# Layer 3's input halves stored by quarter as [w, sample], and the result read back with a step

## The chip, the cores and the metric

The kernel runs on one core of one Trainium2 chip. A core has five engines with a queue each: PE (TensorE, matrix products into PSUM), DVE (VectorE), ACT (ScalarE), POOL (GpSimd[...]) and SP (SyncE, which here only starts DMA transfers). The metric is the device time of one execution in microseconds. Before the change the median of three runs is 3868.43 us (3868.01 to 3870.23).

## What is computed

The input x has 8192 samples of 8 channels by 16 rows by 16 columns, in f32. Four layers run one after the other; each normalises its input by groups of two channels (`_gn`), applies an operator, and adds the result to its input:

```
x = x + L0(_gn(x))    # a tensor-train operator on [8, 16, 16], plus bias
x = x + L1(_gn(x))    # 3x3 convolution, batch norm over all samples, relu
x = x + L2(_gn(x))    # 3x3 convolution on values rounded to int8 steps, one scale for the whole tensor
x = x + L3(_gn(x))    # 3x3 convolution with binarized weights, edge padding
```

The change touches layer 3 alone:

```
w = binarize(weight)                  # sign(weight) * mean(|weight|) of its output channel
xp = pad(x, 1 on each side, mode='edge')
out = conv(xp, w) + bias
```

"Edge" padding means that the column left of column 0 repeats column 0, and the column right of column 15 repeats column 15.

## The kernel before

**Layout.** A tile holds 128 samples. Its 128 partitions are the pairs (channel, row), 8 x 16, and its 2048 words per partition are [sample b, column w], with w innermost. So there are 64 tiles. A convolution over channels and rows is a product with a 128x128 banded matrix, and its three column offsets are three products that add up in one PSUM bank. A bank holds 512 f32 words per partition, which is a quarter of a tile: 32 samples by 16 columns (`NQ = 4`, `QS = 32`, `BANK = 512`).

**Stages.** Four passes go over all tiles: layer 0 with the convolution of layer 1 (to about 2650 us), the batch norm and the statistics of layer 2 (to about 3090 us), and then layer 2's convolution together with layer 3 (from about 3095 us to the end). The change lies in the last pass. All engine instructions go through helper `InOrder`, which keeps them in the order in which the program text issues them, so each engine is a strict list; the profile shows the helper's line, L43, for all of them, and rows are told apart by the names of their tiles.

**The last pass, one turn of its loop** (lines 969 to 989; names of tiles in brackets as the profile shows them). Each turn works on several tiles at different depth:

- PE: six products of layer 2 for the first half of a tile [pq], products that spread small statistics over all partitions [ps_a, ps_r, ps_o], six more for the second half [pq], sixteen that sum x and x squared [s], then 24 of layer 3 [pf]: twelve for the first half of the tile and twelve for the second. The twelve are two quarters, times two operands, times three column offsets.
- DVE: small statistics [diag_d, rows_d, mr, diag_e, rows_e], `finish` of the second half of layer 3 [reads pf], layer 2's addition [reads pq], `scale2` [v], the reduction of s and small steps [s_d, mv], `scale3` [t, which lives in the buffers sq and xh], `finish` of the first half of the next tile [reads pf].
- ACT: x squared [sq], the offset [c], layer 2's second half [bs<-pq], `edges3` [lo<-lo], `round2` [q<-v], `high3` [hi<-xh, hi<-sq], its edges [hi<-hi], `bias2` [bias].
- POOL: the second half of layer 2 added to x [<-bs], a power of four words [mv<-mv,mhalf], `low3` [lo<-sq,hi and lo<-xh,hi], and the offset added to x [<-c].

**How layer 3 feeds PE.** The scaled input t is split in two operands for PE: `high3` rounds t to the type fp32r [hi], and `low3` stores what is left, t - hi [lo]. Each has 18 columns per sample, [128 samples, 18], so that columns 0 and 17 can hold the repeated edges, which `edges` fills with 2 x 128 words. `layer3` then reads, for column offset n, 32 runs of 16 words that lie 18 words apart (`tv[:, :, n:n + W]`), and `finish` adds the PSUM result, times `scale3`, to x with one DVE instruction of 1024 words per half. The PSUM tiles [pc] of layers 2 and 3 come from one pool with two buffers, in turn: pq of the first half, pq of the second half, pf of the first half, pf of the second half. A product into a buffer waits until the engine that reads it, DVE or ACT, has read what it held. hi, lo and t have two buffers each; sq holds one square at a time.

Of the kernel before, what the change touches and what calls it, by code (L numbers as in the profile page):

```python
# [8 lines left out]
F32 = mybir.dt.float32  # L9
F32R = mybir.dt.float32r  # L10
# [3 lines left out]
ALU = mybir.AluOpType  # L14
# [4 lines left out]
P = 128  # L19
C, H, W = 8, 16, 16  # L20
# [4 lines left out]
NQ = 4  # L25
QS = P // NQ
BANK = QS * W
# [26 lines left out]
def tile_net(ctx: ExitStack, tc: tile.TileContext, xb, xt_in, pack0, pack1, pack2, out):  # L54
# [3 lines left out]
    pe, dve, act, pool = (InOrder(tc, e) for e in (nc.tensor, nc.vector, nc.scalar, nc.gpsimd))  # L58
# [74 lines left out]
    L = {}  # L133
# [129 lines left out]
    def samples(t):  # L263
        return t.rearrange("p (b w) -> p b w", w=W)

    def over_w(stat, a, b):

        return stat[:, a:b].unsqueeze(2).to_broadcast([P, b - a, W])
# [25 lines left out]
    with first as s:  # L294
        small = s.enter_context(tc.tile_pool(name="small1", bufs=3))
        wk = s.enter_context(tc.tile_pool(name="wk", bufs=2))
# [4 lines left out]
        T = [dict() for _ in range(NT)]  # L301
# [263 lines left out]
        for n in range(NT * NQ):  # L565
            t, q = divmod(n, NQ)
# [58 lines left out]
        t = NT - 1  # L625
# [83 lines left out]
    with tc.tile_pool(name="p2", bufs=2) as p2, tc.tile_pool(name="ps2", bufs=2, space=PSUM) as ps2:  # L709
        T = T2  # L710
# [115 lines left out]
    with ExitStack() as s:  # L826
        wk = s.enter_context(tc.tile_pool(name="wk3", bufs=2))
# [5 lines left out]
        T = [dict() for _ in range(NT)]  # L833
# [17 lines left out]
        def halves(t):  # L851
            return t.rearrange("p (h n) -> p h n", h=2)
# [70 lines left out]
            T[i]["t"] = t  # L923


        def edges(t):
            act.copy(t[:, :, 0:W + 2:W + 1], t[:, :, 1:W + 1:W - 1])

        def high3(i):
            T[i]["hi"] = hi = wk.tile([P, P, W + 2], F32R, name=f"hi_{i}", tag="hi")  # L930
            act.copy(hi[:, :, 1:W + 1], samples(T[i]["t"]))
            edges(hi)

        def low3(i):
            hi = T[i]["hi"]
            T[i]["lo"] = lo = wk.tile([P, P, W + 2], F32R, name=f"lo_{i}", tag="lo")
            pool.tensor_tensor(lo[:, :, 1:W + 1], samples(T[i].pop("t")), hi[:, :, 1:W + 1].bitcast(F32), ALU.subtract)
            x = samples(T[i]["x"])
            pool.tensor_tensor(x, x, over_w(T[i].pop("c"), 0, P), ALU.add)

        def edges3(i):
            edges(T[i]["lo"])

        def layer3(i, h):
            pc = ps_c.tile([P, 2, BANK], F32, name=f"pf_{i}_{h}", tag="pc")
            for m, t in enumerate(("hi", "lo")):
                for k in range(2):
                    q = 2 * h + k
                    tv = T[i][t][:, q * QS:(q + 1) * QS]
                    for n in range(3):  # L950
                        pe.matmul(samples(pc[:, k]), L["sign3"][:, n], tv[:, :, n:n + W],
                                  start=(m == n == 0), stop=(m == 1 and n == 2))
            T[i]["pf", h] = pc

        def finish(i, h):
            x = halves(T[i]["x"])[:, h]
            pc = T[i].pop(("pf", h)).rearrange("p k n -> p (k n)")
            dve.scalar_tensor_tensor(x, pc, L["scale3"], x, ALU.mult, ALU.add)
            if h == 1:
                nc.sync.dma_start(out[order[i]], T[i]["x"])  # L960
                T[i].clear()
# [7 lines left out]
        for i in range(-FIRST, NT + 4):  # L969
            at(i + AHEAD, lambda j: j >= AHEAD and load3(j))  # L970
            at(i + FIRST, rows2)
            at(i - 1, rows3)
            at(i - 3, finish, 1)
            at(i, square3)
            at(i + 1, layer2, 0)
            spread(i + FIRST, i - 1)
            at(i - 1, offset3)
            at(i + 1, layer2, 1)
            at(i + FIRST, scale2)
            at(i, stats3)  # L980
            at(i - 1, scale3)
            at(i - 2, edges3)
            at(i + 2, round2)
            at(i - 1, high3)
            at(i + 2, bias2)
            at(i - 1, low3)
            at(i - 2, layer3, 0)
            at(i - 2, finish, 0)
            at(i - 2, layer3, 1)
# [69 lines left out]
```

## Time and profile before

| what | value |
|---|---|
| median of three runs | 3868.43 us |
| span of the profiled execution | 3866.3 us |
| PE, DVE, ACT, POOL busy over the span | 3616.3, 3408.0, 2510.8, 3044.2 us |
| steady part of the last pass | 3123 to 3838 us, 715 us |
| PE, DVE, ACT, POOL busy in it | 710.89, 657.07, 554.13, 695.93 us |
| granted TensorE clock in it | 1.00 |
| share of the DMA engines' time in it | 0.43 |
| one turn of the loop (one tile) | 11.55 us (layer 3's products start at 3399.89, 3411.44, 3422.99 us) |

How to read it: matrix products are pipelined, so the time that the profile gives to one (433 ns) is not its share of PE's time; the distance from one start to the next is. A column "idle before" gives how long an engine stood still ahead of a group of instructions and whose end it waited for. A loop in which each engine has a fixed list settles to the length of its slowest cycle of waits, and that cycle may run through several engines.

### The profile page before, as it was taken

The page shows a single profiled execution, that of the slowest core. Times are in us where ns is not written, and L with a number is a line of the kernel's source. Part 1 is how long each engine was busy: PE and PEld are TensorE (multiplying, and loading weights), DVE is VectorE, ACT ScalarE, POOL GpSimd, SP SyncE. Part 2 cuts the span into 40 slices and gives each one's busy share as a digit, 9 for nine tenths or more (in the row PEclk, how much of TensorE's full clock was granted, in tenths as well). Part 3 has the DMA queues.
Part 4 walks back from the last instruction along what each step waited for, and adds up shares of the span by engine and source line. Part 5 has one row for each costly group of instructions (what it writes and reads, how often), then busy time and mean ns, then how long its engine had stood idle before and what let it go on. Part 6 is the DMA issues. An engine that isn't in the chain of part 4 may idle for free.

```text
span 3866.3 us, 52820 instructions
## 1 busy us (share of the span) xinstructions
PE 3616.3 (94%) x16326; PEld 2131.0 (55%) x16326; DVE 3408.0 (88%) x6316; ACT 2510.8 (65%) x2672; POOL 3044.2 (79%) x3101
## 2 busy tenths in 40 slices
PE   7899999999999999999999999996665589999998
PEld 4566666666666666666666666662211145555555
DVE  6988888888888888888888888877998889999997
ACT  4566666666666666666666666665665477777775
POOL 4687777777777777777777777766887679999998
PEclk8999999999999999999999999998776699999999
DMA  5678788787887878878788787757999624444432
GB/s 206 208 249 269 254 264 269 250 268 254 264 270 250 269 253 263 269 252 265 255 263 269 254 265 255 257 185 283 425 424 425 280 90 183 185 183 183 180 153 98
DMA packets 210665, 960.93 MB, mean 249 GB/s; under 512 B 44880, under 2 KB 45136, under 8 KB 109776
## 3 DMA queue, kind: packets, MB, share of 16 engines
q1 hardware_dynamic: 173664, 692.22, 48.3%
q0 software_dynamic: 36288, 264.26, 22.9%
q8 instruction: 131, 2.15, 0.2%
q14 instruction: 150, 1.23, 0.1%
q10 hardware_dynamic: 432, 1.08, 0.1%
HBM read 578.84 MB, written 378.54 MB: 248 GB/s over the span
## 4 chain that ended last, share of the span: by engine, by line
PE 84%; DVE 7%; DMA 4%; issue 2%; POOL 1%; ACT 1%; POOLq 0%; DVEq 0%; SPq 0%; ACTq 0%
PE po L43 44%; PE pu L43 12%; PE pf L43 10%; PE pm L43 6%; PE pq L43 4%; PE s L43 3%; PE pc L43 3%; DVE top L43 3%; DMA yk<-y_d 1%; DVE ys L43 1%; DMA x_d<-xs 1%; DMA x_d<-xk 1%; DMA xk<-x_d 1%; DMA xs<-x_d 1%; DMA u<-x_d 1%
## 5 line engine op out<-in xcount | busy, mean ns | idle before, releaser
L43 PE MATMUL po<-u,core 128*128 128x512 f32 (+1 forms) x4112 | 1847.0, 592 | 1.9 <-DVE xs L43 1.9
L43 ACT COPY u<-pu 128x2048 f32<-128x2048 f32 x512 | 955.4, 1866 | 534.1 <-PE pu L43 534.0
L43 PEld LDWEIGHTS po<-u,core 128*128 128x128 f32 x4112 | 745.7, 190 | 740.4 <-issue 737.3
L43 PE MATMUL pu<-core2r,xl 128*128 128x256 f32 x4032 | 680.1, 311 | 11.3 <-DMA xl<-limb_d 11.3
L43 PEld LDWEIGHTS pu<-core2r,xl 128*128 128x128 f32 x4032 | 529.2, 189 | 134.1 <-issue 133.8
L43 POOL TENSOR_TENSOR bs<-bs,xh 128x512 fp32r<-128x512 f32 (+1 forms) x253 | 324.6, 1283 | 206.0 <-ACT xh L43 206.0
L43 POOL TENSOR_TENSOR v<-e 128x128 f32<-128x128 f32 x750 | 397.4, 541 | 0.0
L43 DVE TENSOR_TENSOR xs<-po,xs 128x512 f32<-128x512 f32 x256 | 177.0, 691 | 236.6 <-PE po L43 236.6
L43 ACT ACTIVATE m<-pm,b 128x128 f32<-128x128 f32 x250 | 91.7, 367 | 405.4 <-PE pm L43 405.4
L43 PEld LDWEIGHTS pm<-v,fast 128*128 128x128 f32 x2000 | 263.4, 192 | 129.9 <-issue 112.1
L43 POOL TENSOR_TENSOR e<-x1n,x 128x512 f32<-128x512 f32 x250 | 305.9, 1224 | 23.4 <-ACT x L43 16.1
L43 DVE TENSOR_TENSOR bs<-bs,stat 128x1024 f32<-128x1024 f32 x252 | 290.8, 1216 | 2.1
L43 POOL TENSOR_TENSOR xs<-xs,w 128x2048 f32<-128x2048 f32 x64 | 291.5, 4555 | 0.0
L43 PE MATMUL pm<-v,fast 128*128 128x128 f32 x2000 | 264.9, 276 | 9.6 <-DVE ends L43 9.6
L43 ACT ACTIVATE x<-x1n 128x512 f32<-128x512 f32 x500 | 246.9, 544 | 2.1 <-DVE x1n L43 2.1
L43 POOL TENSOR_TENSOR mv<-mv,mhalf 128x4 f32<-128x4 f32 x127 | 130.8, 1030 | 146.4 <-DVE mv L43 146.4
L43 PE MATMUL pf<-hi,sign 128*128 128x512 f32 x768 | 226.8, 433 | 0.0
L43 PE MATMUL pf<-lo,sign 128*128 128x512 f32 x768 | 219.5, 423 | 3.3 <-ACT lo L43 3.3
L43 POOL DMA_DIRECT2D xl<-limb_d x252 | 149.7, 594 | 87.5 <-ACT x L43 47.8
L43 POOL TENSOR_TENSOR v<-r 128x128 f32<-128x128 f32 x500 | 215.6, 447 | 0.0
L43 POOL TENSOR_TENSOR mvb<-mvb,mhalf 128x4 f32<-128x4 f32 x64 | 66.3, 1035 | 179.4 <-DVE mvb L43 174.6
L43 ACT ACTIVATE sq<-xs 128x2048 f32<-128x2048 f32 (+1 forms) x107 | 199.3, 1862 | 4.6 <-POOL xs L43 4.6
(289 smaller groups left out, 7180.4 us busy)
## 6 DMA issues: line engine op xcount, KB each, us to landing
xl<-limb_d POOLq DMA_DIRECT2D x252, 1024.0 KB, 7.4
x_d<-xs SPq DMA_DIRECT2D x76, 1024.0 KB, 8.4
bs<-in_xb SPq DMA_DIRECT2D x64, 1024.0 KB, 5.7
xs<-in_xt SPq DMA_DIRECT2D x64, 1024.0 KB, 7.6
limb_d<-xh SPq DMA_DIRECT2D x1008, 64.0 KB, 4.3
limb_d<-bs SPq DMA_DIRECT2D x1008, 64.0 KB, 5.1
y_d<-ys SPq DMA_DIRECT2D x60, 1024.0 KB, 8.0
u<-x_d SPq DMA_DIRECT2D x36, 1024.0 KB, 6.1
```

The source lines that it names most:

```text
L43: return self.tc.keep_in_program_order(op(*args, **kwargs))
```

## The change

The operands hi and lo are stored by quarter as [18 columns, 32 samples] in place of [128 samples, 18 columns]. A column offset n is then a shift by 32 n words, so that each product reads one run of 512 words. To get there, `high3` and `low3` read t with a step of 16 words (samples innermost) and write runs. The products' columns come out in the order [w, b], so `finish` reads PSUM with a step of 32 words to bring them back to [b, w]; it does so with one instruction per quarter, where it had one per half. The edges become runs of 32 words.

```diff
         def high3(i):
-            T[i]["hi"] = hi = wk.tile([P, P, W + 2], F32R, name=f"hi_{i}", tag="hi")
-            act.copy(hi[:, :, 1:W + 1], samples(T[i]["t"]))
+            T[i]["hi"] = hi = wk.tile([P, NQ, W + 2, QS], F32R, name=f"hi_{i}", tag="hi")
+            act.copy(hi[:, :, 1:W + 1], by_w(T[i]["t"]))
             edges(hi)
...
+        def by_w(t):
+            return t.rearrange("p (q b w) -> p q w b", q=NQ, w=W)
...
-            T[i]["lo"] = lo = wk.tile([P, P, W + 2], F32R, name=f"lo_{i}", tag="lo")
-            pool.tensor_tensor(lo[:, :, 1:W + 1], samples(T[i].pop("t")), hi[:, :, 1:W + 1].bitcast(F32), ALU.subtract)
+            T[i]["lo"] = lo = wk.tile([P, NQ, W + 2, QS], F32R, name=f"lo_{i}", tag="lo")
+            pool.tensor_tensor(lo[:, :, 1:W + 1], by_w(T[i].pop("t")), hi[:, :, 1:W + 1].bitcast(F32), ALU.subtract)
...
-                    tv = T[i][t][:, q * QS:(q + 1) * QS]
                     for n in range(3):
-                        pe.matmul(samples(pc[:, k]), L["sign3"][:, n], tv[:, :, n:n + W],
+                        tv = T[i][t][:, q, n:n + W].rearrange("p w b -> p (w b)")
+                        pe.matmul(pc[:, k], L["sign3"][:, n], tv,
                                   start=(m == n == 0), stop=(m == 1 and n == 2))
...
-            pc = T[i].pop(("pf", h)).rearrange("p k n -> p (k n)")
-            dve.scalar_tensor_tensor(x, pc, L["scale3"], x, ALU.mult, ALU.add)
+            pc = T[i].pop(("pf", h)).rearrange("p k (w b) -> p k b w", w=W)
+            for k in range(2):
+                v = samples(x[:, k * BANK:(k + 1) * BANK])
+                dve.scalar_tensor_tensor(v, pc[:, k], L["scale3"], v, ALU.mult, ALU.add)
```

## The prediction

> **What bounds the kernel now.** I read the stretches first, since only the last pass changes, then the chain of waits inside it, the rows by shape and last the waits. In a steady stretch of 100 us (columns: length, then busy time of PE, weight loads, DVE, ACT and POOL, clock, DMA share, GB/s):
>
> ```profile
> 3400.00:3500.00 100.00, 100.00 (x496) 59.28 (x497) 93.28 (x168) 77.39 (x69) 97.55 (x36) 1.00 0.47 179
> ```
>
> Three engines are nearly full. The chain of waits shows which ends last (start, length, what):
>
> ```profile
> 3399.89 6.42 PE pf L43 x24
> 3406.31 1.31 PE pq L43 x6
> 3407.62 0.22 PE ps_a L43 x2
> 3407.84 0.22 PE ps_r L43 x2
> 3408.07 0.22 PE ps_o L43 x2
> 3408.29 1.30 PE pq L43 x6
> 3409.59 1.85 PE s L43 x16
> 3411.44 6.42 PE pf L43 x24
> ```
>
> It is PE end to end: 6.42 + 1.31 + 3 x 0.22 + 1.30 + 1.85 = 11.54 us, the whole turn. A pf product takes 6.42 / 24 = 267 ns, a pq product, with as many columns, 1.31 / 6 = 218 ns. So PE has something to gain. The waits of 3200 to 3800 us (52 turns) say how much room the others leave:
>
> ```profile
> ACT hi L43 <- DVE xh L43: 59.4, 26, 2.3
> ACT hi L43 <- DVE sq L43: 59.4, 26, 2.3
> ...
> POOL lo L43 <- POOL mv L43: 14.6, 53, 0.3
> ...
> DVE mr L43 <- POOL mv L43: 12.3, 52, 0.3
> DVE s_d L43 <- PE s L43: 12.0, 51, 0.2
> ```
>
> POOL stands still for 14.6 / 53 = 0.27 us a turn, DVE for 12.3 / 52 + 12.0 / 51 = 0.47 us. So POOL's own list takes 11.55 - 0.27 = 11.28 us and DVE's 11.55 - 0.47 = 11.08 us. POOL's wait is named after mv, which POOL itself had finished. In order of time its lo starts at 3405.85 us, and hi's copy on ACT ends at 3405.73: the wait is for ACT. ACT waits 2.3 us a turn for DVE's t, so it has room, but its copy sits on a path: t, hi, lo.
>
> [...]
>
> ```profile
> L43 DVE TENSOR_REDUCE mod<-ident 128x32 f32<-128x128 f32 x1 | 0.4, 375 | 0.0
> ...
> L43 DVE TENSOR_REDUCE grp<-ident 128x4 f32<-128x128 f32 x1 | 0.3, 275 | 0.0
> ```
>
> mod reads 128 words with a step of 32 words, grp reads as many in a run: (375 - 275) / 128 = 0.78 ns a word more. [...] POOL's r<-x1n steps by 16 bytes on both inputs and takes 445 ns for 128 words, v<-r, which steps nowhere, 447.
>
> **The change part by part, for one turn.**
>
> *PE.* 24 products go from 267 to about 218 ns (the pq row). [...] eight pu products of 256 columns take 0.94 us in the chain of the first pass, 118 ns each[...]. Saved: 24 x 0.049 = 1.18 us. PE's list falls to 10.36 us. This lies on the path that sets the end, but only until the next list binds.
>
> *DVE, finish.* Two instructions of 1024 words become four of 512:
>
> ```profile
> L43 DVE SCALAR_TENSOR_TENSOR xs<-pf,scale,xs 128x1024 f32<-128x1024 f32 x32 | 40.3, 1260 | 0.0
> ```
>
> A word costs 1.03 ns (bs<-bs,stat takes 1216 ns for 1024 words, ys<-ys,stat 687 for 512), so 512 words less leave 733 ns; two of these, less 0.09 us of overlap (the two v of 1213 ns take 2.34 us together), are 1.38, so 0.1 us more a half and 0.2 a turn. Then the step: 2048 words a turn are read from PSUM 128 bytes apart. No row of this trace reads PSUM so. Bounds: nothing, if PSUM gives any word at full rate[...]. I take the 0.78 ns of the mod row[...]: 2048 x 0.78 = 1.60 us. Queued behind finish are the next additions, v, the reduction and t, all of DVE's list; PE's second pq waits for the second finish too, since that frees its PSUM buffer. DVE's list: 11.08 + 0.2 + 1.6 = 12.88 us.
>
> *ACT, high3.* 2048 words read with a step of 64 bytes, written in runs. The edges row has single words on both sides:
>
> ```profile
> L43 ACT CAST hi<-hi 128x256 fp32r<-128x256 f32 x52 | 28.2, 543 | 1.7
> ```
>
> From u<-pu (1866 ns for 2048 words) and m<-pm (258 for 128) a word costs 0.84 ns and an instruction 151. Edges are then (543 - 151) / 256 = 1.53 ns a word, 0.69 over, for two stepped sides. For one stepped side I take 0.5 ns, so 1.0 us more on 1.93. Ends: nothing, and 1.9 us (the core<-cps copy, written with a step: (1054 - 151) / 512 = 1.76 ns a word, 0.93 over). ACT's 2.3 us of waiting hold the work, but not the path through hi. The two edges become runs and may save 0.14 us each (256 x 0.84 + 151 = 366 at best); ACT waits after them, so I count nothing.
>
> *POOL, low3.* One input with a step. By the r row nothing[...]. I take 0: POOL's list stays at 11.28 us.
>
> *The path through hi.* pow on POOL, DVE's mr to t, ACT's hi, then POOL's lo, the addition of c, that of bs and the next pow but one: from the end of pow at 3405.59 to the pow that ends two turns on it is 2 x 11.55 = 23.10 us, with only DVE's 0.23 us wait for s in it, so 22.87. One finish lies on it (0.1 + 0.8 us) and one hi (1.0): 24.77 / 2 = 12.39 us a turn. That is less than DVE's 12.88.
>
> *Sum.* The longest is DVE: 12.88 - 11.55 = 1.33 us more a turn, times 62 turns (715 / 11.55) = 82 us. At the end, where the engines no longer overlap, two slower finishes and one hi (about 3 us) stand against pf groups shorter by 0.6 us each: 1 us. Forecast: 3868 + 83 = 3951 us. The 1.18 us of PE are lost whole, since PE then waits for DVE.
>
> **The rivals.**
>
> *B: PSUM gives stepped words at full rate.* [...] Then DVE's list is 11.28, but the path through hi is (22.87 + 0.1 + 1.0) / 2 = 11.98: 0.43 x 62 = 27 us more, 3895 us. With hi at its upper end 12.43, 3923 us. [...]
>
> *C: no step costs anything.* For it: POOL's r row, and that 18-word rows do not slow DVE's or ACT's copies. The path through hi gives (22.87 + 0.1) / 2 = 11.49, POOL and DVE 11.28: 0.06 x 62 = 4 us less, 3865 us; if the rows without gaps also shorten hi and lo a little, down to POOL's and DVE's 11.28, 3868 - 0.27 x 62 = 3852 us. So even with the whole of PE's gain the others allow no more than 0.4%. Against it: mod, edges and core, three rows on two engines that all pay.
>
> *D: the PSUM step costs as the worst SBUF case.* [...]
>
> **How the numbers follow.** Forecast A (DVE pays 0.6 to 1.1 ns a word, 3929 to 3992 us) 0.60, B 0.20, C 0.12, D 0.08. The predicted time is A's, 3951 us. The range leaves out C and D, 0.2, and so runs from B's lower part, 3884, to A's upper end, 3992. Faster by over 0.2% (under 3860.7) is the better half of C: 0.06. Within 0.2% is the rest of C with a B of small costs: 0.07. Slower: 0.87.
>
> **What the changed profile would show.** Right: pf near 218 ns a product in the chain and PE no longer full; finish as four rows of 512 words near 733 + 400 = 1.13 us; DVE above 98% in the steady stretch and the chain through DVE; hi near 2.9 us; lo near 4.27. Wrong: finish at about 0.73 us a row (then B or C, told apart by hi)[...]; pf still at 267 ns (then the 18-word rows were not what slowed it). What would make the time wrong most is the price of a stepped PSUM word, which stands in no row.

## The result, and the profile after

The changed kernel takes 3966.52 us (3965.61 to 3967.03, four runs), the kernel before 3868.95 us: a ratio of 1.0252, interval 1.0234 to 1.0269. It is slower by 98 us, and 3966.5 lies in the range that was given. The main reason that was given for it, a slower DVE, does not hold, as the rows show at once. The steady stretch first, in the same columns as before:

```profile
3400.00:3500.00 100.00, 88.11 (x450) 50.49 (x448) 84.23 (x162) 83.05 (x62) 96.86 (x32) 1.00 0.42 161
```

PE is no longer full, as forecast. But DVE, which the forecast had above 98%, fell from 93 to 84: it does hardly more work per turn, in a longer turn. ACT rose from 77 to 83, and POOL is the fullest engine, without being full. The rows by shape of 3200 to 3800 us (to the right of the bar: us in all, mean ns of one, and idle time before):

```profile
L43 PE MATMUL pf<-hi,sign 128*128 128x512 f32 x556 | 149.7, 404 | 0.0
...
L43 POOL TENSOR_TENSOR lo<-xh,hi 128x2048 fp32r<-128x2048 f32 x24 | 134.5, 5606 | 9.3 <-POOL mv L43 9.3
...
L43 ACT CAST hi<-sq 128x2048 fp32r<-128x2048 f32 x23 | 86.7, 3771 | 28.7 <-DVE sq L43 28.7
...
L43 DVE SCALAR_TENSOR_TENSOR u<-pf,scale,u 128x512 f32<-128x512 f32 x64 | 44.4, 734 | 3.9 <-POOL u L43 3.9
```

finish takes 734 ns for 512 words that lie 128 bytes apart in PSUM, just what the forecast had worked out for words without a step (733). hi and lo were these before:

```profile
L43 POOL TENSOR_TENSOR lo<-xh,hi 128x2048 fp32r<-128x2048 f32 x26 | 111.0, 4268 | 7.2 <-POOL mv L43 7.2
...
L43 ACT CAST hi<-sq 128x2048 fp32r<-128x2048 f32 x26 | 50.2, 1932 | 59.4 <-DVE sq L43 59.4
```

So hi grew from 1.93 to 3.77 us and lo from 4.27 to 5.61. The waits of the changed kernel in the same stretch (46 or 47 turns):

```profile
DVE mr L43 <- POOL mv L43: 69.5, 46, 1.5
...
ACT hi L43 <- DVE sq L43: 28.7, 23, 1.3
ACT hi L43 <- DVE xh L43: 28.6, 23, 1.3
POOL lo L43 <- POOL mv L43: 18.3, 47, 0.4
```

DVE now stands still for 1.51 us a turn until POOL's power is done (0.24 before), so DVE is not the bound. POOL stands still for 18.3 / 47 = 0.39 us ahead of lo (put down to mv, but, as before, lo starts just after hi's end on ACT): its own list is not the whole turn either. What joins the two is seen in order of time (start, length, engine, what; in brackets the idle time before it):

```profile
3402.76 1.01 POOL L43 TENSOR_TENSOR mv<-mv,mhalf 128x4 f32<-128x4 f32 x1
3403.80 0.16 DVE L43 TENSOR_TENSOR mr<-ps_a,mv 128x4 f32<-128x4 f32 x1 [1.52 <-POOL mv L43]
...
3410.87 2.34 DVE L43 TENSOR_TENSOR sq<-xk,ps_r 128x1024 f32<-128x1024 f32 x2
...
3413.24 3.76 ACT L43 CAST hi<-sq 128x2048 fp32r<-128x2048 f32 x1 [1.23 <-DVE sq L43]
...
3417.14 5.58 POOL L43 TENSOR_TENSOR lo<-sq,hi 128x2048 fp32r<-128x2048 f32 x1 [0.36 <-POOL mv L43]
...
3422.68 3.69 POOL L43 TENSOR_TENSOR xk<-xk,c 128x2048 f32<-128x2048 f32 x1
...
3426.33 2.41 POOL L43 TENSOR_TENSOR ys<-ys,bs 128x1024 f32<-128x1024 f32 x1
...
3428.70 1.02 POOL L43 TENSOR_TENSOR mv<-mv,mhalf 128x4 f32<-128x4 f32 x1
```

Read it as one path: the power ends at 3403.77, mr starts 0.03 us later, DVE works through its list to t (here in sq), hi starts as t ends (3413.21 to 3413.24), lo starts 0.14 us after hi ends (17.00 to 17.14), the additions of c and bs follow without a gap, and the next power of this path runs from 3428.70 to 3429.72. From end of power to end of power that is two turns, 25.95 us, 13.0 a turn. It is the forecast's "path through hi", which it had put second.

Over 3300 to 3600 us the starts of lo lie 13.00 us apart (11.55 before). The last power of all starts at 3840.54 us before and 3933.03 after: 92.5 us of the loss lie ahead of it, 64 turns of 1.45 us. The rest of the loss, 6 us, lies behind it, where the last two hi and lo have nothing to hide behind (25.8 us from there to the end before, 31.8 after).

### The profile page after: what moved, and what is told of

Same layout as the page of the kernel before. It is cut to its first block, busy times and chain, and to the rows that moved or that the text cites. A ratio compares the mean times of both kernels' runs of the same rounds, so it can differ in the third digit from the quotient of the medians.

```text
span 3964.8 us, 53012 instructions
## 1 busy us (share of the span) xinstructions
PE 3614.8 (91%) x16326; PEld 2130.1 (54%) x16326; DVE 3422.0 (86%) x6444; ACT 2616.4 (66%) x2672; POOL 3128.9 (79%) x3101
## 4 chain that ended last, share of the span: by engine, by line
PE 65%; DVE 19%; DMA 6%; ACT 4%; issue 3%; POOL 3%; DVEq 0%; POOLq 0%; SPq 0%; ACTq 0%
PE po L43 43%; PE pu L43 12%; PE pm L43 6%; ACT hi L43 4%; DVE v L43 3%; PE pc L43 3%; DVE top L43 2%; DVE sq L43 2%; DVE xh L43 2%; POOL mv L43 2%; DMA yk<-y_d 2%; DVE u L43 1%; DVE xs L43 1%; DVE s_d L43 1%; DVE ys L43 1%
## 5 line engine op out<-in xcount | busy, mean ns | idle before, releaser
L43 PE MATMUL pq<-q,band 128*128 128x480 bf16 (+1 forms) x768 | 188.8, 382 | 40.7 <-DVE xs L43 11.6
L43 PE MATMUL pf<-hi,sign 128*128 128x512 f32 x768 | 209.9, 409 | 0.4 <-ACT hi L43 0.4
L43 PE MATMUL pf<-lo,sign 128*128 128x512 f32 x768 | 202.1, 399 | 6.5 <-ACT lo L43 6.5
```

Of the source, the lines that this page charges most:

```text
L43: return self.tc.keep_in_program_order(op(*args, **kwargs))
```

## The experiments

**The theory, P.** The turn is the longest of these: the path through hi, (22.87 + what finish, hi and lo grow by) / 2; POOL's list, 11.28 us plus the growth of lo; DVE's list, 11.28 with finish in four pieces; PE's list. For the changed kernel the path gives (22.87 + 0.1 + 1.84 + 1.34) / 2 = 13.08 us, and 13.00 was measured. (In other runs too this sum comes out up to 0.1 us a turn too long; why stays open, and differences of that size are not read from it.) The main rival is the recorded forecast, that stepped words from PSUM slow DVE; the others are named with each run. "Turn" is the mean distance of lo's starts from 3300 to 3600 us.

### Are stepped words from PSUM what costs?

```diff
-            pc = T[i].pop(("pf", h)).rearrange("p k (w b) -> p k b w", w=W)
+            pc = T[i].pop(("pf", h)).rearrange("p k (b w) -> p k b w", w=W)
```

> The changed kernel, but finish reads PSUM in the order in which the products wrote it, so layer 3's result is added to x in the wrong order of words. Theory P (the path through hi sets the turn, a stepped PSUM word costs DVE nothing): no change, 3966 us within 4, and the finish rows stay near 734 ns for 512 words. Rival D (the forecast on record: stepped PSUM words slow DVE and DVE sets the turn): 2048 words x 0.78 ns less on DVE, 1.3 us a turn, about 3885 us.

3966.8 us, ratio to before 1.0256 (1.0242 to 1.0270), as the changed kernel; turn 13.00 us. The row without the step:

```profile
L43 DVE SCALAR_TENSOR_TENSOR u<-pf,scale,u 128x512 f32<-128x512 f32 x64 | 44.4, 735 | 4.3 <-POOL u L43 4.3
```

735 ns without, 734 with a step of 128 bytes: the step costs DVE nothing here. The recorded forecast's mechanism is out.

### The steps of hi and lo, one at a time and together

`own_order` reads t in its own order (`"p (q w b) -> p q w b"`, which has the shape of `by_w` but no step) and leaves the rest of the change in place. The words then come to lie elsewhere than the change wants them, so these runs are prices of a part, not kernels.

```diff
-            act.copy(hi[:, :, 1:W + 1], by_w(T[i]["t"]))
+            act.copy(hi[:, :, 1:W + 1], own_order(T[i]["t"]))
```

> The changed kernel, but high3 reads t in its own order, so that hi holds the words in the wrong places. Theory P: hi falls from 3.77 to about 1.9 us, the path through hi is (22.87 + 0.1 + 1.34) / 2 = 12.16 us a turn and POOL's list, 11.28 + 1.34 = 12.62, takes its place: 0.4 us less than the 13.01 of the changed kernel, times 65 turns, about 3941 us. Rival Q (POOL's list with the slower lo sets the turn alone and hi waits on nothing that matters): no change, 3966 us.

3935.26 us, ratio 1.0174 (1.0160 to 1.0188). hi falls to 1.91 us, the turn to 12.55, and POOL is full:

```profile
3400.00:3500.00 100.00, 91.37 (x464) 53.45 (x464) 86.88 (x169) 70.40 (x64) 100.00 (x33) 1.00 0.44 166
```

So hi's step costs 1.86 us on ACT (3.77 against 1.91), which was never full, and the time falls by 31 us all the same, because hi lies on the path. Then POOL's list takes over (12.62 by the theory).

```diff
-            pool.tensor_tensor(lo[:, :, 1:W + 1], by_w(T[i].pop("t")), ...
+            pool.tensor_tensor(lo[:, :, 1:W + 1], own_order(T[i].pop("t")), ...
```

> The changed kernel, but low3 reads t in its own order, so that lo is not t minus hi. Theory P: lo falls from 5.61 to about 4.2 us, POOL's list to 11.28, the path through hi to (22.87 + 0.1 + 1.84) / 2 = 12.41 us a turn, 0.6 less: about 3927 us. Rival Q (POOL's list alone): back to about 11.5 us a turn, 3868 us.

3937.47 us, ratio 1.0181 (1.0167 to 1.0195), turn 12.57 us: 10 us more than P expected, and far from rival Q's 3868. The row says why:

```profile
L43 POOL TENSOR_TENSOR lo<-xh,hi 128x2048 fp32r<-128x2048 f32 x24 | 109.9, 4579 | 23.4 <-POOL mv L43 23.4
```

Without the step lo takes 4.58 us, not the 4.27 of before: on POOL, runs of 512 words are 0.31 us slower than the rows of 16. With that, the path is (22.87 + 0.1 + 1.84 + 0.31) / 2 = 12.56 us, as measured. Of lo's 1.34 us, then, 0.31 are the new layout and 1.03 the step. POOL waits 46.7 us over 48 turns here, nearly 1 us a turn, and is no bound: the path is.

Both edits together:

> The changed kernel, but high3 and low3 both read t in its own order, so that layer 3 gets its samples and columns in the wrong places; products, edges and finish are those of the changed kernel. Theory P: both steps are the whole loss; what is left is the path through hi, (22.87 + 0.1) / 2 = 11.49 us a turn, and PE's gain can't be had: 3865 us within 5, no more than 0.3% from the kernel before. Rival R (something else of the change costs as well, finish or the edges): over 3880 us. Rival G (PE's shorter list would be worth its 0.8 us a turn if the steps were free): about 3815 us.

3870.97 us, ratio 1.0007 (0.9999 to 1.0015), turn 11.55 us. Without the two steps nothing of the loss is left; finish in four pieces and the new edges cost nothing that shows. But neither is there a gain from PE's shorter list, although pf keeps the changed kernel's rows of 404 ns (433 before). POOL is busy for 100.00 us of 100 here: with lo at 4.57 us its list is 11.28 + 0.30 = 11.58 us, as long as the turn before. The new layout itself, then, takes back on POOL what it gives PE.

### The path or POOL's list?

In the next two runs POOL's power comes ahead of the addition of bs in POOL's list; everything is still computed. That takes the addition, 2.4 us, out of one of the two turns of the path, and leaves the length of POOL's list alone.

```diff
                 act.activation(z, pc, AF.Identity, bias=L["bias2"], scale=inv)
-                pool.tensor_tensor(x, x, z, ALU.add)
+
+        def add2(i):
+            x = halves(T[i]["x"])[:, 1]
+            pool.tensor_tensor(x, x, z3[i % 2], ALU.add)
...
             at(i, stats3)
+            at(i + 1, add2)
```

> The changed kernel, with POOL's power of four words moved ahead of the addition of bs in POOL's list; everything is computed. Theory P (a path over two turns, from the end of the power through DVE, hi and lo to the next power but one): the addition of bs, 2.4 us, leaves one of the two turns of that path, which falls to about (26.15 - 2.4) / 2 = 11.9 us, and POOL's list, 11.28 + 1.34 = 12.62, sets the turn: 0.4 us less, about 3941 us. Rival Q (POOL's list is what sets it already): no change, 3966 us.

On the changed kernel: 3940.43 us, ratio 1.0183 (1.0169 to 1.0197), turn 12.60 us. A move of four words' work ahead of another instruction gives 26 us back. Nothing was made faster, so the path set the turn, and now POOL's list (12.62) does:

```profile
3400.00:3500.00 100.00, 92.91 (x460) 52.18 (x464) 86.31 (x168) 84.06 (x65) 99.96 (x33) 1.00 0.43 165
```

> The kernel before, with the same move in POOL's list; everything is computed. Theory P: PE's list of 11.54 us sets the turn before the change and stays: no change, 3868 us within 4. Rival H (the path through hi was what set the turn before the change too): about 0.2 us a turn less, 3855 us.

On the kernel before: 3868.18 us, ratio 0.9998 (0.9990 to 1.0006), turn 11.55 us. DVE's wait for the power is gone, PE stays full (100.00 us of 100), and the time does not move: before the change PE's list set the turn, as the forecast said.

> The changed kernel with high3 and low3 reading t in its own order (layer 3 gets its words in the wrong places) and POOL's power moved ahead of the addition of bs. Theory V (with the steps gone, POOL's list sets the turn: lo takes 4.57 us in runs of 512 words, 0.30 more than in the kernel before, so the list is 11.28 + 0.30 = 11.58): no change against the same kernel without the move, 3871 us within 4. Rival P2 (the path through hi still sets it): 0.2 us a turn less, about 3858 us.

On the changed kernel with both steps left out: 3868.56 us, ratio 0.9998 (0.9990 to 1.0006), turn 11.52 us. That is 2.4 us less than without the move, and the ranges of the two overlap; a gain of 0.2 us a turn is excluded. So POOL's list, not the path, takes PE's gain there.

### One part alone: finish by quarter, and the products alone

```diff
-            pc = T[i].pop(("pf", h)).rearrange("p k n -> p (k n)")
-            dve.scalar_tensor_tensor(x, pc, L["scale3"], x, ALU.mult, ALU.add)
+            pc = T[i].pop(("pf", h))
+            for k in range(2):
+                v = x[:, k * BANK:(k + 1) * BANK]
+                dve.scalar_tensor_tensor(v, pc[:, k], L["scale3"], v, ALU.mult, ALU.add)
```

> The kernel before, with finish in one instruction per quarter of 512 words, as the change has it, and nothing else; everything is computed. Theory: DVE's list grows by 0.2 us to 11.28, under PE's 11.54: no change, 3869 us within 4. Rival (DVE's waits for POOL and PE leave no room): up to 0.2 us a turn more, 3882 us.

3868.82 us, ratio 1.0000 (0.9991 to 1.0008): the two extra instructions a turn hide in DVE's slack.

```diff
-                    tv = T[i][t][:, q * QS:(q + 1) * QS]
+                    tv = T[i][t][:, q * QS:(q + 1) * QS].rearrange("p b w -> p (b w)")
                     for n in range(3):
-                        pe.matmul(samples(pc[:, k]), L["sign3"][:, n], tv[:, :, n:n + W],
+                        pe.matmul(pc[:, k], L["sign3"][:, n], tv[:, n * QS:n * QS + BANK],
```

> The kernel before, but the products read one run of 512 words at a shift of 32 words from hi and lo as the kernel before stores them, so layer 3's products get the wrong words; copies, edges and finish stay. This is PE's part of the change alone. Theory V (PE has no more to give than the next lists allow): pf near 233 ns instead of 267, PE's list 10.7 us, the path through hi 22.87 / 2 = 11.44 us a turn, 0.1 less: about 3862 us. Rival G (PE's list sets the turn alone): 10.7 us a turn, about 3815 us.

3858.22 us, ratio 0.9970 (0.9958 to 0.9981), turn 11.34 us (the path's sum was 11.44). This is all that PE's part is worth by itself: 11 us, 0.3%, since the path comes next.

> The same as PE's part of the change alone, with POOL's power moved ahead of the addition of bs as well (wrong words in layer 3's products). Theory V: the path through hi loses one addition, POOL's list of 11.28 us sets the turn, 0.27 us less than before: about 3851 us. Rival U (DVE's list with its waits holds the turn at 11.44): 3862 us.

3849.29 us, ratio 0.9950 (0.9937 to 0.9962), turn 11.22 us, with POOL full:

```profile
3400.00:3500.00 100.00, 98.34 (x512) 59.66 (x519) 94.70 (x168) 81.10 (x72) 100.00 (x37) 1.00 0.50 190
```

This is the end of what shorter products can bring here: with layouts that cost nothing and the path out of the way, POOL's list of 11.2 us stops it at 20 us. (In these two runs layer 3 reads other words than the reference needs, so they are prices, not kernels.)

### A smaller step

If only the size of the step costs, a layout with a step of 8 bytes should keep most of PE's gain. hi and lo as [64 pairs of samples, 18 columns, 2] (the edit of hi; lo, the products and finish follow it):

```diff
+        def by_pair(t):
+            return t.rearrange("p (g c w) -> p g c w", c=2, w=W)
+        def inner(t):
+            return t[:, :, 1:W + 1].rearrange("p g w c -> p g c w")
...
-            act.copy(hi[:, :, 1:W + 1], samples(T[i]["t"]))
+            act.copy(inner(hi), by_pair(T[i]["t"]))
```

> The kernel before, with hi and lo stored as [pair of samples, 18 columns, 2 samples]: a product reads 16 runs of 32 words, high3 and low3 read t in runs and write with a step of 2 words, finish reads PSUM with a step of 2 words in two instructions a half; everything is computed. Theory S ([...]a step of 8 bytes costs little): pf near 235 ns, hi near 2.4 us, lo near 4.3, the path through hi (22.87 + 0.1 + 0.5) / 2 = 11.7 us a turn: 3868 + 0.2 x 65 = 3880 us. Rival T (any step over one word costs ACT and POOL what 64 bytes cost): 3966 us.

3891.95 us, ratio 1.0057 (1.0045 to 1.0070), turn 11.88 us. Better than the changed kernel by 75 us, slower than before by 22, and 12 us more than was expected. The products stand 245 ns apart (six start 1.47 us after the six before), for 235 expected. hi took 2.32 us, a little less than expected, but lo more:

```profile
L43 POOL TENSOR_TENSOR lo<-sq,hi 128x2048 fp32r<-128x2048 f32 x26 | 125.8, 4837 | 3.4 <-POOL mv L43 0.5
...
L43 ACT CAST hi<-sq 128x2048 fp32r<-128x2048 f32 x26 | 60.4, 2322 | 62.2 <-DVE sq L43 62.2
```

With lo's 0.57 us and hi's 0.39, the path is (22.87 + 0.1 + 0.39 + 0.57) / 2 = 11.97 us, for 11.88 measured. A step of 8 bytes is cheaper here (hi's 0.39 us against 1.84, lo's 0.57 against 1.34), but not free. (hi and lo write with it, where the changed kernel reads with its step; so two layouts are compared, not the size of a step alone.)

> The pairs layout and the power first, together; everything is computed. Theory P with S: the path through hi loses one addition and no longer sets the turn, PE's list is near 10.7 us, POOL's 11.28 us is the longest: 0.27 us a turn less than before, about 3852 us, faster than both kernels. Rival U (another path, such as DVE's list with its waits for POOL, holds the turn at 11.5): 3868 us.

3884.56 us, ratio 1.0041 (1.0027 to 1.0055), turn 11.77 us. The forecast of 3852 us failed, and rival U's reason does too: DVE is not the bound. POOL is:

```profile
3400.00:3500.00 100.00, 97.45 (x500) 56.17 (x499) 92.84 (x176) 79.34 (x69) 100.00 (x35) 1.00 0.47 179
```

The expectation took POOL's list as 11.28 us, with lo as before. In order of time:

```profile
3303.16 1.11 POOL L43 TENSOR_TENSOR mv<-mv,mhalf 128x4 f32<-128x4 f32 x1
3304.15 2.46 POOL L43 TENSOR_TENSOR xs<-xs,bs 128x1024 f32<-128x1024 f32 x1
3306.49 4.92 POOL L43 TENSOR_TENSOR lo<-xh,hi 128x2048 fp32r<-128x2048 f32 x1
3311.27 3.79 POOL L43 TENSOR_TENSOR xs<-xs,c 128x2048 f32<-128x2048 f32 x1
3314.93 1.11 POOL L43 TENSOR_TENSOR mv<-mv,mhalf 128x4 f32<-128x4 f32 x1
```

The rows overlap, so the distance from start to start counts, as with matrix products: 0.99 + 2.34 + 4.78 + 3.66 = 11.77 us. lo takes 4.78 us in that measure, for 4.22 before, and the other three take no longer than before. The slower lo is the whole of what the expectation missed. No version that computes everything beat the kernel before.

## Why the prediction was right or wrong

The time was right within its range and the sign with it; the mechanism was wrong. The second step below needs two rows by shape of the kernel before:

```profile
L43 PE MATMUL pq<-q,band 128*128 128x480 bf16 x416 | 123.9, 380 | 0.0
...
L43 PE MATMUL pq<-q,band 128*128 128x512 bf16 x208 | 79.6, 383 | 0.0
```

By its own steps:

- *What bounds the kernel now:* right. PE's list set the turn (moving the power changed nothing, shorter products gave 11 us), POOL had 0.27 us of room and DVE 0.47.
- *PE, "24 products go from 267 to about 218 ns":* the direction holds, the size was off. Six products start 1.40 us apart from the next six in order of time, 233 ns each, so 0.8 us were saved and not 1.18. The 218 ns came from a misread row. A pq product does not have "as many columns": two of three have 480 (the rows above), so 218 ns is the time of 491 columns on average, and does not show what 512 take. The forecast's other row had the size: pu's 118 ns for 256 columns, doubled, give an estimate of 235 for 512, and 233 came. PE's list is about 10.7 us. "Until the next list binds" holds: the products alone brought 11 us.
- *DVE, finish:* the two extra instructions were sized right (734 ns for 733). **This is the step that failed: "I take the 0.78 ns of the mod row".** The words 128 bytes apart in PSUM cost nothing here (734 against 735 ns for 512). The 0.78 ns was an estimate from a row that reads SBUF; that it holds for PSUM was not shown. (The mod row is no clean price for SBUF either: it writes 32 results where grp writes 4.) With it fell "DVE's list: 12.88 us" and case A. PE's gain was lost whole, as forecast, but not to a full DVE: DVE itself waits for POOL's power. The forecast's own sign of being wrong, "finish at about 0.73 us a row", is what came.
- *ACT, high3:* "1.0 us more" was 1.84, close to the upper end of 1.9 (0.9 ns a word). The edges row, from which 0.5 ns was argued, was no guide; the core<-cps copy (0.93) was.
- *POOL, low3:* "I take 0" was 1.34. The r row has a step of 16 bytes; at 64 bytes the step costs 1.03 us, 0.5 ns a word. Another 0.31 us come with the layout, runs in place of rows of 16 words 18 apart. A row of the kernel before takes as long: the addition xs<-xs,w, 2048 words without gaps, 4555 ns.
- *The path through hi:* right in form, and the step that explains the result once hi and lo have their measured sizes. At the forecast's sizes it gave 12.39 us, with lo's growth put at nothing; at the measured ones it gives 13.08 (13.00 measured).
- *The cases:* what came is rival B, with both of its unknown costs at once, hi's near its upper end (1.84 of 1.9 us) and lo's at 1.34 us. The forecast gave B 0.20 and 3895 us, with hi's cost at 1.0 us and lo's at nothing; together on one path the measured ones give 13 us a turn. That A's 3951 lies near 3966 is chance: a wrong 1.60 us on DVE stood in for 1.84 + 1.34 us on a path of two turns. A's 0.6 to 1.1 ns a word was an estimate around mod's 0.78; D's price of a stepped word stands in no row. C's rows of 18 words were indeed no burden for DVE and ACT: x1n<-x1n,stat, in such rows, takes 1221 ns for 1024 words, bs<-bs,stat without gaps 1216, and ACT's hi 1932 ns into such rows and 1912 in runs.

## What to carry to other kernels

Here the order of words that saved PE 0.8 us a turn cost ACT 1.84 us and POOL 1.34 us to make. Put the price of every stepped read and write next to the gain, from a row of the same engine, the same memory and a step of the same size. When no list is full, look for a path that runs through several engines over more than one turn, and add up what the change lengthens on it; hi's 1.84 us on ACT, an engine with 2.3 us of waiting a turn, was not hidden. And ask what the relieved engine's gain can reach before the next list binds: here 0.3%, and 0.5% with the path opened, with layouts that cost nothing.

## What the runs showed of the hardware

- DVE reads f32 words from PSUM 128 bytes apart at the rate of a run: 734 against 735 ns for 512 words (scalar_tensor_tensor, the other input and the output in runs in SBUF).
- ACT's copy pays 0.91 ns a word to read f32 from SBUF 64 bytes apart (3771 against 1912 ns for 2048, both written in runs) and 0.19 ns to write with a step of 8 bytes (2322 against 1932 ns in rows of 16).
- POOL's subtraction pays 0.50 ns a word for one input 64 bytes apart (5606 against 4579 ns), and with everything in runs it is slower than with hi and lo in rows of 16 words 18 apart (4579 against 4268 ns). Why was not tried.
- PE's fp32r products of 512 columns need 267 ns with rows of 16 words and 233 with one run, at a granted clock of 1.00. The bf16 products beside them need 218 for 491 columns on average, 0.44 ns a column where the run takes 0.46. With runs of 32 words the products stand 245 ns apart. What makes the rows of 16 take 34 ns more than the run was not shown.
- POOL's rows can look longer than they are. Where POOL never waits, the power of four words is shown with up to 1201 ns, for 1022 before, but each row starts before the last has ended: from start to start it takes 0.99 us, and the addition of c 3.65 to 3.66 us, as before.
